# Ring products of channel pairs on two row tiles, the automaton beside its own image's map, and VectorE's gate operations behind a step's taps

## The chip, the cores and the metric

The kernel runs on one core of a Trainium2 chip. A core has TensorE (PE in the profile; PEld are its weight loads), VectorE (DVE), ScalarE (ACT), GpSimd (POOL) and SyncE (SP), and 16 DMA engines. POOL and SP issue the copies here. The metric is the device time of one launch in microseconds (us); lower is better.

## The reference

An input of 32 images, 8 channels, 256 x 256, f32, goes through four layers, each `x = x + layer(norm(x))`. Only layer 0 is touched by the change. With `g` the normalised image it is:

```python
# automaton: a map that is smoothed with a 3x3 kernel per channel, 15 times
grid = drive = g
for _ in range(15):
    mapped = 3.9 * grid * (1.0 - grid)
    local = conv(mapped, K_local, groups=8)
    physics = 0.7 * mapped + 0.3 * local
    grid = 0.85 * physics + 0.15 * drive
cml = clip(grid, 0.0001, 0.9999)
# the map: 3x3 convolution to 128 hidden channels, then 1x1 back to 8
h = relu(conv(g, Wp, bp))
nca = sigmoid(conv(h, Wu, bu))
# the gate: 3x3 convolution of all 24 channels to 8, then 1x1
gin = concatenate([g, cml, nca])
q = sigmoid(conv(relu(conv(gin, Wg1, bg1)), Wg2, bg2))
out = q * cml + (1.0 - q) * nca
```

Layer 1 is a quantized 3x3 convolution (its scale needs the largest value over the whole result of layer 0), layer 2 a plain 3x3 convolution, layer 3 a 5x5 box filter.

## The kernel before, in words

**Layout of the automaton.** Six channels of an image run on TensorE. An image is cut into patches of 16 x 8 pixels, with the 128 pixels of a patch on the partitions and the 512 patches in the free dimension. One step of one channel is two products that add up in one PSUM tile `psc`. `patch_sb` (L391, 128 rows) takes the neighbours inside a patch, and `ring_sb` (L393, 80 rows) those outside it. The 80 ring rows lie in the tile `rings`: the neighbours to the left and right (16 rows each), and for the rows above and below three shifted copies of 8 rows each (24 and 24). They are copied from the tile `state` by four copies on SP (`spread`, L259). VectorE adds the drive (L402, the eviction of a `psc`), and ScalarE squares into `state` (L419). The six channels go in two halves of three, each half with its own `state` and `rings`, and three `psc` buffers in all.

The other two channels run on VectorE in the tile `strip`, with rows of the image on the partitions: nine multiply-adds of 128 x 1024 a step (L338, "taps"; three after the first half's evictions, six after the second's), then L412 and L413. Two copies (`edges`, L263 and L264) exchange the border rows through SP.

**The map and the gate.** `gated()` makes one image's map in 32 batches (`NCH` = 8 blocks n of 4 batches). A batch is four products `ph` from column tiles `im` (L633, evicted to `hh` on ScalarE in L638) and, one batch late, four products of 32 columns into four column strips of `pn` (L610). `im` is loaded from the padded image `xn_d` in DRAM by six copies on POOL a batch (L505), four batches ahead. For each block a gate follows: three groups of products into `pg` (L531, L539 for rows of neighbouring blocks, L543), a ReLU, a product `pq` (L548), a sigmoid into `gt` (L550), and seven VectorE operations (L561 to L568), after which POOL writes the result to `x1_d` (L569). The map's output `nh` stays in SBUF in a ring of eight rows; the gate's halo rows of it are copied from there.

**Order.** The instructions of each engine run in the order in which the program writes them (`manual_schedule`). The automaton of image b (`lattice`) and the map with the gates (`gated`) are generators. Each `yield` of the lattice names a gap in units of about one microsecond of TensorE work, and the loop draws as much work from `gated()`. A step has two halves with 6.3 units each (`BLOCK`). What is drawn beside image b's automaton is the map and the gates of image b - 1. So the first automaton has no map beside it, and the map and gates of the last image run after the last automaton. A third generator, `errands`, writes and loads images and takes the next image's statistics, one piece a half step.

Of the kernel before, what the change touches and what calls it, by code (L numbers as in the profile page):

```python
# [39 lines left out]
    (32, 8, (RB - 1) * PW, 1, -1 - SY, 3, SY),  # L40
    (56, 8, 0, 1, 1 - SY, 3, SY),
)
RING = 80
# [3 lines left out]
HALF = CP // 2  # L47
RQ = 4
BLOCK = 6.3
# [17 lines left out]
def kernel(  # L67
# [100 lines left out]
    with ExitStack() as es:  # L168
# [9 lines left out]
        ring_sb = const(wt, ring, [RING, CP, P], "ring_sb")  # L178
# [41 lines left out]
        nh = wt.tile([P, 8, WP], F32, name="nh")  # L220
        zero = wt.tile([C, WP], F32, name="zero")
        states = [wt.tile([P, HALF, SN], F32, name=f"state{i}") for i in range(2)]
        rings = [wt.tile([RING, HALF, SN], F32, name=f"rings{i}") for i in range(2)]
# [4 lines left out]
        for t in (*xbs, nh, zero, strip):  # L228
            nc.gpsimd.memset(t, 0.0)
        for t in (*states, *rings):  # L230
            nc.gpsimd.memset(t, 0.25)
# [5 lines left out]
        nr_d = [dram.tile([P, HB, WP], F32, name=f"nr_d{i}") for i in range(3)]  # L237

        cr_d = [dram.tile([P, HB, WP], F32, name=f"cr_d{i}") for i in range(3)]
        for t in xn_d:  # L240
            nc.sync.dma_start(
                window(t, 0, [[HP * WP, C], [(HP - 1) * WP, 2], [1, WP]]),
                nh[0:C, 0:2, :],
            )

        def inner(c):

            return states[c // HALF][:, c % HALF, AT : AT + TX * SY].rearrange("p (x y) -> p x y", y=SY)[:, :, 0:TY]

        def spread(half):  # L250

            long = (HALF - 1) * SN + RN
            state = states[half]
            row = state.ap[0][0]
            to = rings[half].rearrange("p c n -> p (c n)")
            for q, n, p, step, far, m, by in RINGS:
                at = p * row + AT + far
                dims = [[step * row, n]] + ([[by, m]] if m > 1 else []) + [[1, long]]
                nc.sync.dma_start(to[q : q + n * m, 0:long], window(state, at, dims))  # L259
# [6 lines left out]
        def errands(b):  # L266
# [3 lines left out]
            if b >= 0:  # L270
                xb = xbs[b % 2]
                for r in four:
                    nc.gpsimd.dma_start(
                        window(
                            xn_d[b % 3], (1 + r.start) * WP,
                            [[HP * WP, C], [RB * WP, HB], [1, 4 * WP]],
                        ),
                        xb[:, r, :].rearrange("p r w -> p (r w)"),
                    )
                    yield  # L280
# [47 lines left out]
        def lattice(b, ahead):  # L328
# [8 lines left out]
            def tap(dy, dx):  # L337
# [8 lines left out]
            nc.vector.tensor_scalar(  # L346
                flat.rearrange("p (x r w) -> p r x w", x=TX, r=RB),
                xi.rearrange("p r (x w) -> p r x w", w=PW),
                st[:, 0:1], st[:, 1:2], ALU.subtract, ALU.mult,
            )  # L350
            yield 5
            for t4 in range(TX // 4):
# [6 lines left out]
                if t4 == 0:  # L359
                    nc.vector.tensor_scalar(  # L360
                        xi, xi, st[:, 0:1], st[:, 1:2], ALU.subtract, ALU.mult
                    )
                if t4 == 4 and b > 0:
                    store(b - 1)
                if t4 == 1:
# [4 lines left out]
                    edges()  # L370
                yield 1
            dr = flat.rearrange("p (x c y) -> p c x y", x=TX, c=C)
            for c in range(CP):
                nc.scalar.activation(inner(c), dr[:, c], AF.Square, bias=minus)
# [3 lines left out]
                if c == 0:  # L378
                    nc.scalar.mul(d2, d2, BETA_)
                if c % HALF == HALF - 1:  # L380
                    spread(c // HALF)
                yield 1.5
            yield 4
            for step in range(STEPS):
                for half in range(2):
                    mine = range(HALF * half, HALF * half + HALF)
# [272 lines left out]
        with tc.manual_schedule():  # L659
# [15 lines left out]
            for _ in rest:  # L675
                pass
# [366 lines left out]
```

## Time and profile before

| what | value |
|---|---|
| median of 3 runs | 16326.91 us (16326.64 to 16338.44) |
| the profiled execution | 16318.33 us, span 16316.6 us |
| mean granted TensorE clock | 0.961 |
| PE, DVE, ACT, POOL busy | 95%, 72%, 35%, 34% of the span |
| DMA | 2276 MB, 1057742 packets |
| start of the first and of the last image's automaton | 33.8 and 12927.2 us |

The busy share of an engine is an average over very different stages. Layer 0 takes the first 13593 us, the other layers the rest, and within layer 0 the first automaton and the last map have stages of their own. A busy PE isn't a PE at its peak, as records overlap: what a product costs is read from the starts of records that follow each other. Idle time of an engine that isn't the bound costs nothing.

### The profile page before, as it was taken

To read this page: it belongs to the slowest core of one execution; us is meant where nothing else is said; L and a number is where in the kernel's file an instruction comes from. 1 tells how busy PE (TensorE), PEld (TensorE's weight loads), DVE (VectorE), ACT (ScalarE), POOL (GpSimd) and SP (SyncE) were. 2 spreads that over 40 slices of the span, in tenths; PEclk is the share of its full clock that TensorE was granted. 3 is DMA by queue.
4 is the path that set the end of the run, shared out by engine and by line. 5 is a ranking of instruction groups with operands and counts; after the bars stand their busy time and mean duration, and the time that the engine had idled before them with its cause. 6 is when DMAs were issued, how large, how long until landed. Compare 5 with 4: busy or idle time off the path is not lost.

```text
span 16316.6 us, 141125 instructions
## 1 busy us (share of the span) xinstructions
PE 15452.2 (95%) x42888; PEld 6215.7 (38%) x42888; DVE 11705.9 (72%) x14652; ACT 5726.7 (35%) x8862; POOL 5598.2 (34%) x9491
## 2 busy tenths in 40 slices
PE   6999999999999999999999999999999997999999
PEld 2333333333333333333333333333333332333333
DVE  7777777777777777777777777777777764555554
ACT  2433444443434434443434444343444442111110
POOL 1333333333333333333333333333333342111111
PEclk7999999999999999999999999999999998999999
DMA  4766666666666666666666666666666664555554
GB/s 104 148 146 144 150 147 144 147 150 146 149 144 148 150 147 147 144 147 145 147 142 149 148 144 147 141 148 146 147 149 147 146 134 98 119 119 119 119 118 105
DMA packets 1057742, 2276.12 MB, mean 139 GB/s; under 512 B 419740, under 2 KB 623508, under 8 KB 1050724
## 3 DMA queue, kind: packets, MB, share of 16 engines
q0 software_dynamic: 704512, 1492.80, 40.6%
q1 hardware_dynamic: 352484, 774.29, 23.4%
q8 instruction: 356, 5.83, 0.2%
q14 instruction: 390, 3.19, 0.1%
HBM read 1078.04 MB, written 471.38 MB: 95 GB/s over the span
## 4 chain that ended last, share of the span: by engine, by line
PE 74%; DVE 13%; DMA 7%; ACT 3%; issue 2%; SPq 1%; POOL 0%; DVEq 0%; ACTq 0%; POOLq 0%
PE ph L633 17%; PE psc L391 14%; PE psc L393 13%; PE pg L531 9%; DVE acc L338 7%; PE psv L725 5%; PE pn L610 5%; PE psv L811 4%; DMA qb<-qh 3%; DMA rings<-state 2%; PE psv L729 2%; PE pq L548 1%; PE pg L543 1%; PE pg L539 1%; DVE psc L402 1%
## 5 line engine op out<-in xcount | busy, mean ns | idle before, releaser
L338 DVE SCALAR_TENSOR_TENSOR acc<-strip,taps_sb,acc 128x1024 f32<-128x1024 f32 x3840 | 4930.4, 1284 | 124.8 <-DMA strip<-strip 4.7
L505 POOL DMA_DIRECT2D im<-xn_d x6144 | 3458.3, 566 | 3250.0 <-PE ph L633 1434.7
L633 PE MATMUL ph<-im,wp_sb 72*128 72x512 f32 x8192 | 4091.7, 615 | 308.8 <-ACT hh L638 251.3
L638 ACT ACTIVATE hh<-ph,bp_sb 128x512 f32<-128x512 f32 x4096 | 2755.8, 690 | 4441.9 <-PE ph L633 4385.7
L402 DVE SCALAR_TENSOR_TENSOR psc<-psc,flat 128x512 f32<-128x512 f32 x2880 | 1921.4, 696 | 2813.0 <-PE psc L393 2797.2
L391 PE MATMUL psc<-state,patch_sb 128*128 128x512 f32 x5760 | 2812.0, 626 | 74.1 <-ACT state L419 63.3
L393 PE MATMUL psc<-rings,ring_sb 80*128 80x512 f32 x5760 | 2713.5, 607 | 129.8 <-DMA rings<-state 129.8
L633 PEld LDWEIGHTS ph<-im,wp_sb 72*128 72x128 f32 x8192 | 1489.5, 193 | 2425.4 <-issue 1587.8
L419 ACT ACTIVATE state<-psc,minus 128x512 f32<-128x512 f32 x2688 | 1690.2, 690 | 1818.8 <-DVE psc L402 1713.1
L391 PEld LDWEIGHTS psc<-state,patch_sb 128*128 128x128 f32 x5760 | 1114.5, 199 | 1696.2 <-issue 1375.7
L393 PEld LDWEIGHTS psc<-rings,ring_sb 80*128 80x128 f32 x5760 | 1114.7, 194 | 1576.8 <-issue 1545.7
L569 POOL DMA_DIRECT2D x_d<-xc x256 | 146.9, 574 | 3493.1 <-DVE xc L564 3416.6
L811 PE MATMUL psv<-xr,w_sb 128*128 128x512 f32 x2560 | 1162.9, 600 | 1.3 <-DVE xr L792 1.3
L610 PE MATMUL pn<-hh,wu_sb 128*32 128x512 f32 x8192 | 1133.9, 609 | 3.3 <-ACT hh L638 3.3
L776 POOL DMA_DIRECT2D x_d<-x x512 | 321.0, 643 | 1941.0 <-DVE x L770 1696.3
L725 PE MATMUL psv<-xh,w_sb 128*128 128x512 f32 x1536 | 753.0, 629 | 9.6 <-issue 9.6
L531 PE MATMUL pg<-xq,wg_sb 128*128 128x512 f32 x1536 | 749.3, 626 | 0.0
L754 ACT ACTIVATE x<-psv,b_sb,sc 128x512 f32<-128x512 f32 x256 | 199.3, 779 | 1466.2 <-PE psv L729 1465.8
L531 PE MATMUL pg<-cq,wg_sb 128*128 128x512 f32 x1536 | 713.7, 601 | 0.0
L811 PEld LDWEIGHTS psv<-xr,w_sb 128*128 128x128 f32 x2560 | 466.1, 189 | 610.8 <-issue 606.0
L338 DVE SCALAR_TENSOR_TENSOR acc<-strip,taps_sb,d 128x1024 f32<-128x1024 f32 x480 | 613.2, 1277 | 0.0
L831 DVE TENSOR_TENSOR y<-psv,y 128x512 f32<-128x512 f32 x256 | 177.1, 692 | 593.7 <-PE psv L811 593.7
(163 smaller groups left out, 12188.9 us busy)
## 6 DMA issues: line engine op xcount, KB each, us to landing
im<-xn_d POOLq DMA_DIRECT2D x6144, 96.6 KB, 6.6
rings<-state SPq DMA_DIRECT2D x1920, 159.5 KB
rings<-state SPq DMA_DIRECT2D x1920, 106.3 KB
strip<-strip SPq DMA_DIRECT2D x960, 126.0 KB
xn_d<-xb POOLq DMA_DIRECT2D x128, 516.0 KB, 7.7
nr_d<-xb POOLq DMA_DIRECT2D x128, 516.0 KB, 7.2
xq<-nr_d POOLq DMA_DIRECT2D x128, 516.0 KB, 5.1
cq<-cr_d POOLq DMA_DIRECT2D x128, 516.0 KB, 7.9
```

Source lines behind the costliest of these rows:

```text
L338: nc.vector.scalar_tensor_tensor(acc, strip[:, dy : dy + RQ, dx : dx + W], taps_sb[:, 3 * dy + dx : 3 * dy + dx + 1], d2 if dy == 1 and dx ...
L391: nc.tensor.matmul(pss[-1], patch_sb[:, c, :], inner(c), start=True, stop=False)
L393: nc.tensor.matmul(pss[c % HALF], ring_sb[:, c, :], rings[half][:, c % HALF, 0 : TX * SY].rearrange("p (x y) -> p x y", y=SY)[:, :, 0:TY], ...
L402: nc.vector.scalar_tensor_tensor(ps, ps, FLOOR, dr[:, c], ALU.max, ALU.add)
L419: nc.scalar.activation(inner(c), pss[c % HALF], AF.Square, bias=minus)
L505: nc.gpsimd.dma_start(im[24 * dy : 24 * dy + 24, k, 0:run], window(xn_d[b % 3], at, [[HP * WP, C], [1, 3], [1, run]]),)
L531: nc.tensor.matmul(o, wg1_sb[:, s, dx, :], src[:, :, dx : dx + W], start=s == dx == 0, stop=False,)
L610: nc.tensor.matmul(pn[32 * q : 32 * q + 32, :], wu_sb[:, i, :], hh, start=i == 0, stop=i == 3,)
L633: nc.tensor.matmul(ph.rearrange("p (k w) -> p k w", w=W), wp_sb, im[:, :, j * WP : j * WP + W], start=True, stop=True,)
L638: nc.scalar.activation(hh, ph, AF.Relu, bias=bp_sb)
L725: nc.tensor.matmul(o, w[:, dx, :], src[:, 2 * i : 2 * i + 2, dx : dx + W], start=dx == 0, stop=False,)
L811: nc.tensor.matmul(pss[k].rearrange("p (c w) -> p c w", w=W), w3_sb[:, dx, :], xr[:, k, mine, dx : dx + W], start=dx == 0, stop=stop,)
```

## The change

**Ring products.** The rings have no shifted copies any more except for the four corners: 16 + 16 rows (left, right), 8 + 8 (above, below), and four rows for the corners above and below: 56 in all. The rings of channel j lie at partitions 0 to 55 and those of channel j + 3 at 64 to 119 of one tile, and the two products of such a pair follow each other, one from each half of the partitions, into two `psc` tiles. A step has three pairs. Pairs 0 and 1 share `state` and `rings` tiles of set 0, pair 2 has set 1. A set is spread by 12 copies, so a step issues 24.

**Step order.** After a pair's products come its two evictions, two, three or four taps, and small gaps of map work: 0.8 before and 0.8 after the two squares of pairs 0 and 1, 0.8 and 8.6 with pair 2. A step's gaps still add up to 12.6.

**VectorE's gate operations.** They are put into a list `spare` and emitted by `work`: four after a step's last tap, some between the transposes of an image. The write to `x1_d` and an image's statistics follow through `follow()`.

**Own image's map.** The image is normalised in place first, written to `xn_d` at once, and copied to `flat` from there. Image b's map now runs beside image b's automaton, and the gates follow about one image (31 batches) later. `place` holds both back: 28 of an image's batches before the next image begins. The map's output goes through DRAM (`nh_d`), and the gate loads it, like its other inputs, in quarters `nq` with halos.

In the diff a line of "..." marks what is left out.

```diff
 RINGS = (
     (0, 16, PW - 1, PW, -SY, 1, 0),
     (16, 16, 0, PW, SY, 1, 0),
-    (32, 8, (RB - 1) * PW, 1, -1 - SY, 3, SY),
-    (56, 8, 0, 1, 1 - SY, 3, SY),
+    (32, 8, (RB - 1) * PW, 1, -1, 1, 0),
+    (40, 8, 0, 1, 1, 1, 0),
+    (48, 2, (RB - 1) * PW, PW - 1, -1 - SY, 2, 2 * SY),
+    (52, 2, 0, PW - 1, 1 - SY, 2, 2 * SY),
 )
-RING = 80
+RING = 56
+LOW, HIGH = 0, 64
 CP = 6
-HALF = CP // 2
+PAIRS = CP // 2
+SETS = ((0, 2), (2, 1))
-BLOCK = 6.3
+BLOCK = 12.6
...
+        def spread(i):
+            long = (SETS[i][1] - 1) * SN + RN
+            to = rings[i].rearrange("p c n -> p (c n)")
+            for state, base in zip(states[i], (LOW, HIGH)):
+                row = state.ap[0][0]
+                for q, n, p, step, far, m, by in RINGS:
+                    at = p * row + AT + far
+                    dims = [[step * row, n]] + ([[by, m]] if m > 1 else []) + [[1, long]]
+                    nc.sync.dma_start(
+                        to[base + q : base + q + n * m, 0:long], window(state, at, dims)
+                    )
...
-            nc.vector.tensor_scalar(
+            nc.vector.tensor_scalar(xi, xi, st[:, 0:1], st[:, 1:2], ALU.subtract, ALU.mult)
+            nc.vector.tensor_copy(
                 flat.rearrange("p (x r w) -> p r x w", x=TX, r=RB),
                 xi.rearrange("p r (x w) -> p r x w", w=PW),
-                st[:, 0:1], st[:, 1:2], ALU.subtract, ALU.mult,
             )
+            for r in range(0, RB, 4):
+                nc.gpsimd.dma_start(
+                    window(
+                        xn_d[b % 3], (1 + r) * WP, [[HP * WP, C], [RB * WP, HB], [1, 4 * WP]]
+                    ),
+                    xb[:, r : r + 4, :].rearrange("p r w -> p (r w)"),
+                )
...
+            taps_of = (((1, 0), (1, 1)), ((1, 2), (0, 0), (0, 1)), ((0, 2), (2, 0), (2, 1), (2, 2)))
             for step in range(STEPS):
-                for half in range(2):
-                    mine = range(HALF * half, HALF * half + HALF)
+                for j in range(PAIRS):
+                    i = j // 2
+                    mine = (j, PAIRS + j)
...
+                    for ps, base in zip(pss, (LOW, HIGH)):
                         nc.tensor.matmul(
-                            pss[c % HALF], ring_sb[:, c, :],
-                            rings[half][:, c % HALF, 0 : TX * SY].rearrange(
+                            ps, ring_sb[base : base + RING, j, :],
+                            rings[i][base : base + RING, j - SETS[i][0], 0 : TX * SY].rearrange(
                                 "p (x y) -> p x y", y=SY
                             )[:, :, 0:TY],
                             start=False, stop=True,
                         )
...
-                    for dy in (1,) if half == 0 else (0, 2):
-                        for dx in range(3):
-                            tap(dy, dx)
+                    for dy, dx in taps_of[j]:
+                        tap(dy, dx)
...
-                    yield 1.7
+                    yield 0.8
                     if step < STEPS - 1:
-                        for c in mine:
-                            nc.scalar.activation(inner(c), pss[c % HALF], AF.Square, bias=minus)
-                        spread(half)
-                        if half == 1:
+                        for c, ps in zip(mine, pss):
+                            nc.scalar.activation(inner(c), ps, AF.Square, bias=minus)
+                        if j == SETS[i][0] + SETS[i][1] - 1:
+                            spread(i)
+                        if end:
                             edges()
-                    next(ahead, None)
-                    yield BLOCK - 1.7
+                    if end:
+                        work(4)
+                    else:
+                        next(ahead, None)
+                    if j == 1:
+                        follow()
+                    yield BLOCK - 4.0 if end else 0.8
...
+        def work(k):
+            for _ in range(min(k, len(spare))):
+                spare.pop(0)[1]()
+
+        def follow():
+            for n, parts in list(after.items()):
+                if next(parts, True):
+                    del after[n]
...
+                while spare and spare[0][0] <= n - 3:
+                    work(1)
...
-                    for name, t in (("xq", nr_d), ("cq", cr_d)):
+                    for name, t in (("xq", nr_d), ("cq", cr_d), ("nq", nh_d)):
...
+                nc.gpsimd.dma_start(nh_d[b % 3][:, 2 * r2 : 2 * r2 + 2, :], nhs[n % 2])
...
-                due.setdefault(batch + 5, []).append(gate(n, quarter))
+                due.setdefault(batch + BATCHES - 1, []).append(gate(n, quarter))
...
             for b in range(B):
                 ahead = errands(b)
-                for gap in lattice(b, ahead):
-                    if b > 0:
-                        left += gap
-                        while left > 0 and place[0] < b * NCH:
-                            left -= next(rest)
-                        left = min(left, 0.0)
+                place[1] = BATCHES * b - 1
+                for k, gap in enumerate(lattice(b, ahead)):
+                    if b == k == 0:
+                        next(rest)
+                    left += gap
+                    while left > 0 and place[0] < place[1]:
+                        left -= next(rest)
+                    left = min(left, 0.0)
```

In the changed kernel the ring products stand in L410, the patch products in L408, the evictions in L418, L412 and L413 in L428 and L429, and the map's products in L684.

## The prediction

> **What bounds the kernel now.** I read the page's busy shares and slices first, then the time by stages, then the instructions of some 8 us in order of time, and last who waited for whom.
>
> ```profile
> PE 15452.2 (95%) x42888; PEld 6215.7 (38%) x42888; DVE 11705.9 (72%) x14652; ACT 5726.7 (35%) x8862; POOL 5598.2 (34%) x9491
> ...
> PE   6999999999999999999999999999999997999999
> ...
> PEclk7999999999999999999999999999999998999999
> ```
>
> TensorE (PE) is the bound in all but the first slice and one near the end. The time by stages (columns: stretch, its length, busy time and instruction count of PE, PEld, DVE, ACT, POOL, then clock, DMA share, GB/s) shows the first automaton alone, the steady state, and the stretch after the last automaton:
>
> ```profile
> 34.00:389.00 355.00, 227.61 (x459) 96.40 (x460) 286.42 (x304) 73.99 (x114) 29.66 (x46) 0.75 0.43 91
> ...
> 4000.00:8000.00 4000.00, 3852.11 (x10844) 1537.69 (x10842) 3010.68 (x3514) 1600.03 (x2503) 1527.31 (x2628) 0.96 0.67 145
> ...
> 13340.00:13600.00 260.00, 249.28 (x781) 91.55 (x779) 60.34 (x111) 113.02 (x163) 147.07 (x251) 0.98 0.50 121
> ```
>
> In the steady state PE is busy 96% and VectorE (DVE) 75%. The starts of L346, one for each image, run from 33.8 to 12927.2 us: 347.9 us from the first to the second, then 402.7, then 416 to 423. Over the 31 images after the first (the last one ends with its transposes at 13343) the mean is 418.1 us. The map of the last image runs alone to 13593, which is 250 us; layers 1 to 3 take the other 2723.
>
> What one product costs is read from the order of time (columns: start, us, engine, line, operation, count):
>
> ```profile
> 4001.14 2.74 PE L393 MATMUL psc<-rings,ring_sb 80*128 80x512 f32 x6
> ...
> 4003.72 1.02 PE L633 MATMUL ph<-im,wp_sb 72*128 72x512 f32 x2
> ...
> 4004.67 1.07 PE L610 MATMUL pn<-hh,wu_sb 128*32 128x512 f32 x8
> ...
> 4005.66 1.98 PE L633 MATMUL ph<-im,wp_sb 72*128 72x512 f32 x4
> ...
> 4007.58 0.62 PE L539 MATMUL pg<-above,wgh_sb 72*32 72x512 f32 x1
> ...
> 4008.56 1.13 PE L543 MATMUL pg<-nh,wg_sb 128*128 128x512 f32 x2
> ```
>
> Each f32 product is two records, 0.43 us apart (six in 2.58 us: 4001.14 to 4003.72), so 0.86 us. The L610 group, four products in four column strips, holds PE for 0.99 us (4004.67 to 4005.66), not 3.44; the two strips of L539 for 0.98. Its neighbours pay too: L633 to L610 is 0.95 where 0.86 was due, and the four L633 records after it take 1.92, not 1.72, which holds 0.11 for a weight load that isn't ahead and 0.09 for the next switch. So a side-by-side group costs 0.86 + 0.31 us.
>
> **The Trainium skill.** "TensorE: Matmul & The Clock Gate", Part 3 (packing small matmuls), says that products in distinct row groups run concurrently, and gives 3.07 times for four row tiles. "TensorEngine Tiling (Array Packing)", Key Properties, says that a change of tiling mode drains TensorE. The trace agrees for column strips (3.44/1.17 = 2.9 times for four, 0.31 us for switching); it holds no row tiles, so for these the pages are all there is. The same page's "PSUM Bottleneck" warns that what evacuates PSUM may be next: the trace has that margin, below.
>
> **The change, part by part.**
>
> *Ring products.* 2880 products of 80 rows (L393) become 1440 pairs of 56 rows at partitions 0 and 64. An image has 45 pairs. A pair costs 1.72 us now. Side by side: 0.86 + 0.31, and 0.08 for two loads of 128 weight columns (0.19 us each in the rows of L393) in place of 32 (0.11): 1.25. Saved 0.47 x 45 = 21.2 us an image. Bounds: 1.07 (only as much as L539) gives 29; 1.45 (both loads exposed) gives 12.
>
> *Step order.* Three pairs instead of two halves. In a step DVE has 9 taps x 1.284, 6 evictions x 0.697, L412 0.697 and L413 1.227: 17.7 us. The gate's seven operations (0.67 to 0.69 each) now follow a step's taps, four at most: 2.8, in all 20.4. Statistics of the next image add 1.7 in four steps: 22.1. Steps now start 24.3 us apart (mean of the L412 intervals); with 3 x 0.47 less, 22.9. DVE fits, and gate operations no longer stand ahead of evictions, which is what lies behind much of this:
>
> ```profile
> PE ph L633 <- ACT hh L638: 157.1, 77, 4.9
> PE psc L393 <- DMA rings<-state: 65.7, 21, 6.1
> ```
>
> (Waits of PE from 4000 to 12000 us: total, times, longest.) That is 8 us an image that could go; but pairs now stand only 1.6 units of map work (some 1.8 us) apart with three psc buffers, so a late eviction reaches PE sooner. I book 0, with 8 us either way.
>
> *Ring copies.* SP issues 24 a step instead of 8, beside 2 strip copies. Now:
>
> ```profile
> 4003.71 0.83 SPq L263 DMA_DIRECT2D strip<-strip  x1
> ...
> 4007.23 14.55 SPq L259 DMA_DIRECT2D rings<-state  x8
> ...
> L259 SPq DMA_DIRECT2D rings<-state x3840: 549/727/3873, 47.5 to 13302.7; - x192
> ```
>
> An issue takes 0.55 to 0.73 us. New: 24 x 0.6 + 1.6 = 16 of 22.9 us; SP has room. Bytes fall from 160 rows of 6.8 KB a step to 112 of 4.5 or 2.2 KB. The tightest loop is set 0: from pair 0's ring product to pair 1's squares 8.3 us (two ring pairs 2.5, the map work between 1.8, pair 1's patch products 1.7, its evictions 1.4, the last square 0.7, hand-overs 0.2), twelve issues 7.2, landing; then the next step's ring product. In the DMA records the last packet of a half's four copies ends 7.0 us after the last issue (median; 5.4 to 9.5 for 5% to 90%), for copies of 24 rows that move in a file; the new ones have at most 16 rows. With 4 to 7 us the loop takes 19.5 to 22.5 of 22.9: hidden, by little. Booked 0. If that cover went, every us would count 15 times an image.
>
> *POOL.* The gate's third input goes through DRAM: 8 writes and 4 loads of 516 KB an image more, and fewer small halo copies. POOL issues 9536 copies in the program instead of 9472, it is busy 38% of the steady state, and the loads are issued four batches (some 40 us) ahead of use, against landings of 5 to 10 us: 0. DMA share falls by the ring bytes and rises by these: about even.
>
> *Own image's map.* L346 and L360 (2.40 + 2.41 us) change places; the xn_d writes follow. Map columns of the new image are asked for in batch 29 and used in batch 32: behind three or four batches and gate pieces, some 30 us, against 2.4 (normalise) + 2.5 (issue) + 7.7 (landing) + 3.4 (issue) + 6.6 (landing) = 23. Hidden: 0. The first automaton now has 28 map batches beside it: 370 us instead of 347.9, from 8 steps of 23 and 7 of 20.3 (the interval of the lone steps) and some 45 ahead. After the last, 8 gates remain: 8 x 9.65 us of PE is 77, plus 18 for what is left over and some 35 for the first loads and the last chain: 130 instead of 250.
>
> *Sum.* 36 (start) + 370 + 31 x (418.1 - 21.2) + 130 + 2723 = 15563 us of span. The profiled execution took 16318.3 for a span of 16316.6, and the median of the runs is 8.6 above it: 15572, say 15570. Pairs of 1.07 to 1.45 us alone give 15320 to 15850, the 8 us either way 250; taken as independent, 15220 to 15950.
>
> **Rivals.**
> *Half overlap.* A product is two passes, and passes start in order: the second tile's first pass could come with the first tile's second. Three passes: 1.29 + 0.31 = 1.60; 5.4 us saved, images of 412.7, total 16060. Against it: the two L539 products, issued one after the other, start 4007.58 and 4007.59.
> *No overlap (ends slower).* Row tiles take turns, and the switch is still paid: 1.72 + 0.31 = 2.03 a pair, 14 us more an image, 432; with 385 first: 16680. It decides from 1.79 us a pair, where images last 421 and the time is that of before. For it: no row tile in the trace. Against it: the skill, and the column strips.
> *The ring loop on SP (also slower).* Twelve issues at 0.78 and a landing of 9.5 us make the loop 27.2 us a step: 15 x 4.3 more an image, 461, total 17570. It decides from issue and landing of 16 us together (steps of 24.5, images of 421). For it: 26 issues in place of 10 in an in-order queue, strips behind rings. Against it: fewer bytes and no copy of 24 rows.
> *The change does little:* all overlap but stalls of 21 us an image eat it, leaving 0.6% from the two ends (16230).
>
> **Chances.** Main case 0.64, half overlap or stalls of like size 0.14, within 0.2% (what a measurement of this kernel can tell from no change) 0.03, the two slower ones 0.19. Faster 0.78, same 0.03, slower 0.19. The range: 15100 (both favourable bounds at once would be 15070) to 16500, which takes in the second case and the nearest of the slower ones. The main case's own range is 15220 to 15950.
>
> **What would show it.** Right: L410 records start in twos, a pair holds PE some 1.1 us, L428 starts lie near 22.9 us apart, images near 397, PE's waits for rings stay below 10 us an image, and layer 1 starts some 120 us sooner after the last automaton. Wrong: L410 passes in single file; a large "PE psc <- DMA rings"; DVE above 90% with PE waiting for squares; PE waiting for im at an image's start.

## Result, and the profile after

The changed kernel takes 16044.5 us (median of 4 runs, 16013.6 to 16076.6). The kernel before, run beside it, takes 16326.8. The ratio is 0.9827, with a 95% interval from 0.9814 to 0.9839. The forecast was 15570 us: the direction is right and the time lies in the range, but of the 757 us forecast only 282 came.

The profiled execution has a span of 16042.5 us. Its page shows the busy shares, the slices of TensorE and the granted clock:

```profile
PE 15001.2 (94%) x42888; PEld 5437.6 (34%) x42888; DVE 11572.5 (72%) x14652; ACT 5754.6 (36%) x8864; POOL 5667.6 (35%) x9558
...
PE   7999999999999999999999999999999997999999
...
PEclk9999999999999999999999999999999998999999
```

The steady state of the kernel after, by stage (stretch, length, busy time and count of PE, PEld, DVE, ACT, POOL, then clock, DMA share, GB/s):

```profile
4000.00:8000.00 4000.00, 3784.99 (x11025) 1329.06 (x11021) 3027.74 (x3563) 1637.58 (x2546) 1587.12 (x2720) 0.96 0.61 147
```

TensorE does less work, and it is also busy less: 95% of this stretch instead of 96%. The stretch now waits. The order of time shows what a pair costs, and what SyncE does meanwhile:

```profile
4009.72 1.02 PE L408 MATMUL psc<-state,patch_sb 128*128 128x512 f32 x2
4010.67 1.13 PE L410 MATMUL psc<-rings,ring_sb 56*128 56x512 f32 x4
4011.73 1.13 PE L588 MATMUL pq<-g,wg_sb 128*128 128x512 f32 x2
...
4020.47 15.79 SPq L272 DMA_DIRECT2D rings<-state  x23
4020.50 1.13 PE L408 MATMUL psc<-state,patch_sb 128*128 128x512 f32 x2 [0.33 <-ACT state L435]
```

The four records of a pair's two ring products hold TensorE for 1.06 us (4010.67 to 4011.73), and the switch before them adds 0.09 (4009.72 to 4010.67 is 0.95, where two records take 0.86). The two tiles run side by side: in the trace their first records start 0.007 us apart. SyncE, though, spends 15.79 us in one stretch on 23 ring copies, 0.69 us each.

Who waits for that? Waits of PE, DVE and ACT over the whole span (total us, times, longest):

```profile
PE psc L410 <- DMA rings<-state: 212.6, 78, 6.3
...
DVE acc L342 <- DMA strip<-strip: 387.4, 140, 7.7
...
ACT state L435 <- DMA rings<-state: 369.0, 143, 8.7
```

In the kernel before, VectorE waited 4.7 us for strips in all, and ScalarE 85.4 us for ring copies to have read `state`. TensorE's own wait for rings was already there:

```profile
PE psc L393 <- DMA rings<-state: 129.8, 37, 18.9
```

From the starts of TensorE's records one can work out, for 29 images of the steady state, how much of an image is the shortest usual distance between two records (the 15th percentile for each pair of lines; records that start within 0.1 us of each other count as one) and how much is waiting beyond it. The waiting can be put down to the automaton's steps:

| kernel | image, us | products | waiting | step 0 | step 1 | step 3 | step 4 | step 12 | step 13 |
|---|---|---|---|---|---|---|---|---|---|
| before | 418.7 | 385.3 | 33.4 | 8.6 | 6.4 | 0.6 | 0.4 | 7.5 | 0.5 |
| after | 414.0 | 365.3 | 48.7 | 10.4 | 5.6 | 3.3 | 6.4 | 0.6 | 5.3 |

So 20.0 us an image were saved, and 15.3 came back as waiting. Other ways of counting records move this split by some 5 us, but not the image, and hardly the steps. Steps 0 and 1 wait in both kernels. The wait of step 12 has gone, and what is new sits in steps 3, 4 and 13, with about 1 us in most of the others. In steps 3, 4 and 13 VectorE waits 8.3 us an image for strips and ScalarE 7.2 us for ring copies; TensorE's own waits there are mostly for relus and sigmoids that come late, and hardly for rings.

A wait costs more than its length. In this stretch of the changed kernel, TensorE waits for a ring of step 0:

```profile
4154.69 2.04 PE L410 MATMUL psc<-rings,ring_sb 56*128 56x512 f32 x2 [6.32 <-DMA rings<-state]
4156.66 3.78 PE L684 MATMUL ph<-im,wp_sb 72*128 72x512 f32 x4
...
4169.48 1.98 PE L684 MATMUL ph<-im,wp_sb 72*128 72x512 f32 x4
```

```profile
4153.10:4163.20 10.10, 8.51 (x15) 2.38 (x16) 3.17 (x3) 3.11 (x5) 6.60 (x12) 0.50 0.91 258
```

After the wait four L684 records take 3.78 us instead of 1.98, and the granted clock is 0.50 for some 10 us. The traces show such stretches at half clock for 27.5 us an image in the kernel before and 32.2 us in the changed one. As products take twice as long in them, they cost up to half of that; the table counts this as waiting.

### The profile page after: what moved, and what is told of

Its sections match the earlier page's. It is cut to its first block, busy times and chain, and to the rows that moved or that the text cites. A ratio compares the mean times of both kernels' runs of the same rounds, so it can differ in the third digit from the quotient of the medians.

```text
span 16042.5 us, 158554 instructions
## 1 busy us (share of the span) xinstructions
PE 15001.2 (94%) x42888; PEld 5437.6 (34%) x42888; DVE 11572.5 (72%) x14652; ACT 5754.6 (36%) x8864; POOL 5667.6 (35%) x9558
## 5 line engine op out<-in xcount | busy, mean ns | idle before, releaser
L342 DVE SCALAR_TENSOR_TENSOR acc<-strip,taps_sb,acc 128x1024 f32<-128x1024 f32 x3840 | 4925.9, 1283 | 485.2 <-DMA strip<-strip 387.4
L684 PE MATMUL ph<-im,wp_sb 72*128 72x512 f32 x8192 | 4269.2, 635 | 269.3 <-ACT hh L689 126.5
L689 ACT ACTIVATE hh<-ph,bp_sb 128x512 f32<-128x512 f32 x4096 | 2758.0, 688 | 3778.2 <-PE ph L684 3726.1
L418 DVE SCALAR_TENSOR_TENSOR psc<-psc,flat 128x512 f32<-128x512 f32 x2880 | 1871.5, 693 | 2524.4 <-PE psc L410 2517.8
L408 PE MATMUL psc<-state,patch_sb 128*128 128x512 f32 x5760 | 2931.1, 623 | 163.0 <-ACT state L435 157.6
L435 ACT ACTIVATE state<-psc,minus 128x512 f32<-128x512 f32 x2688 | 1723.7, 689 | 3137.9 <-DVE psc L418 2756.2
L684 PEld LDWEIGHTS ph<-im,wp_sb 72*128 72x128 f32 x8192 | 1439.8, 195 | 2677.8 <-issue 1971.7
L410 PE MATMUL psc<-rings,ring_sb 56*128 56x512 f32 x5760 | 1805.7, 650 | 230.9 <-DMA rings<-state 212.6
L408 PEld LDWEIGHTS psc<-state,patch_sb 128*128 128x128 f32 x5760 | 1041.7, 194 | 1904.1 <-issue 1249.6
L410 PEld LDWEIGHTS psc<-rings,ring_sb 56*128 56x128 f32 x5760 | 485.4, 187 | 1436.0 <-issue 1037.1
L571 PE MATMUL pg<-cq,wg_sb 128*128 128x512 f32 x1536 | 772.8, 642 | 0.0
L562 POOL DMA_DIRECT2D xc<-xr_d x256 | 145.7, 569 | 1554.5 <-DVE ext L603 673.2
```

What stands on the lines that cost most here:

```text
L342: nc.vector.scalar_tensor_tensor(acc, strip[:, dy : dy + RQ, dx : dx + W], taps_sb[:, 3 * dy + dx : 3 * dy + dx + 1], d2 if dy == 1 and dx ...
L408: nc.tensor.matmul(pss[-1], patch_sb[:, c, :], inner(c), start=True, stop=False)
L410: nc.tensor.matmul(ps, ring_sb[base : base + RING, j, :], rings[i][base : base + RING, j - SETS[i][0], 0 : TX * SY].rearrange("p (x y) -> ...
L418: nc.vector.scalar_tensor_tensor(ps, ps, FLOOR, dr[:, c], ALU.max, ALU.add)
L435: nc.scalar.activation(inner(c), ps, AF.Square, bias=minus)
L571: nc.tensor.matmul(o, wg1_sb[:, s, dx, :], src[:, :, dx : dx + W], start=s == dx == 0, stop=False,)
```

## Experiments

The theories. **Queue:** 24 ring copies and two strip copies stand one behind another on SyncE; late rings hold TensorE, late strips hold VectorE. **Squares:** ScalarE's order puts relus ahead of a pair's squares, so that `psc` buffers come free late. **Backlog:** VectorE's evictions set the pace. Times are medians. Runs made together share their runs of the kernel before, whose medians lie between 16295 and 16318 us; differences of 30 us between groups mean nothing.

**1. Without the corner copies.** In `spread`:

```diff
-                for q, n, p, step, far, m, by in RINGS:
+                for q, n, p, step, far, m, by in RINGS[:4]:
```

> The eight corner copies of a step (two of the six of each side and each set of pairs) are left out, so that the corner neighbours keep their first value: part of the computation is missing, the matmuls keep their shapes. SyncE issues 16 ring copies a step instead of 24, a third less, and the strip copies stand behind fewer. If the rings' and strips' lateness made the gain small (theory queue): ring products wait 4 us an image instead of 12.8, VectorE waits for strips half as long, squares wait less for the copies that read their state; an image goes from 413.7 to about 404, the kernel to 15700 to 15800. If ScalarE's order did it (theory squares): the second patch product still waits 11 us an image, and the time stays within 50 us of 16045. If VectorE's backlog did it: no change either.

Measured: 15127.7 us, ratio to before 0.9277 (0.926 to 0.9294). That is 917 us less than the changed kernel, three times what theory queue expected. A wait of VectorE, the ring products' group (busy and mean, then idle before them and its releaser) and the steady state of this run:

```profile
DVE acc L342 <- DMA strip<-strip: 11.7, 13, 2.5
```

```profile
L410 PE MATMUL psc<-rings,ring_sb 56*128 56x512 f32 x5760 | 1647.8, 644 | 4.3 <-DMA rings<-state 4.2
```

```profile
4000.00:8000.00 4000.00, 3912.27 (x11879) 1385.88 (x11878) 3288.30 (x3904) 1767.65 (x2748) 1690.01 (x2900) 1.00 0.64 153
```

The waits for rings fall from 212.6 to 4.2 us, those for strips from 387.4 to 11.7; PE is busy 98% and the clock is 1.00. An image takes 382.8 us, with 21.0 of waiting; step 0 has 1.6 instead of 10.4 of it, step 4 has 0.7 instead of 6.4. Two things make the gain larger than the waits of TensorE for rings. What stands behind a late copy waits too: ScalarE's wait for ring copies falls from 369.0 to 65.2 us. And the stretches at half clock fall from 32.2 to 3.2 us an image, which is up to 14.5 of the 31.2 us.

Not all of these 31.2 us are a loss by the change. Step 0 gets shorter by 9.7 us (33.4 to 23.7) and step 1 by 6.3 (29.1 to 22.8), and in the kernel before these two steps lasted 31.4 and 29.5 us. So about half of the gain lies in steps that were as slow before the change.

**2. Ring products not neighbours.** The loop over a pair's channels takes patch and ring product of one, then of the other:

```diff
-                    for c in mine:
+                    for c, base in zip(mine, (LOW, HIGH)):
...
-                    for ps, base in zip(pss, (LOW, HIGH)):
```

> The four products of a pair in another order: patch product and ring product of the first channel, then those of the second. The two ring products are no longer neighbours, so the row tiles cannot run beside each other; copies, buffers and all other orders stay. If the row tiles do overlap and TensorE is what an image waits for: a pair's ring products take 1.72 or more instead of 1.17 us, 0.55 to 0.7 us by 45 pairs = 25 to 31 us an image, time 16800 to 17050. If the image is set by queues and VectorE and TensorE's saving has gone into its own waits (theory queue): less than half comes back, 16200 to 16500. If the tiles had not overlapped: no change.

Measured: 16884.1 us, ratio 1.0354 (1.0328 to 1.0379), 840 us more than the changed kernel and slower than before. In the order of time of this run each product now starts 1.05 us after the one before it:

```profile
4019.64 1.12 PE L410 MATMUL psc<-rings,ring_sb 56*128 56x512 f32 x2
4020.69 1.13 PE L409 MATMUL psc<-state,patch_sb 128*128 128x512 f32 x2
4021.75 1.12 PE L410 MATMUL psc<-rings,ring_sb 56*128 56x512 f32 x2
```

The run takes away more than the overlap: every product pays a change of row tiles, 0.19 us above 0.86. Four products take 4.2 us instead of 2.9, which by 45 pairs would be some 60 us an image; 24 were felt (438.3 against 414.0), as the slower steps gave the copies time: waits for strips fell from 387.4 to 44.6 us. The overlap is real. A run without it whose products do not pay that change each time was not made.

**3. Squares first.** The gap goes behind the squares:

```diff
-                    yield 0.8
                     if step < STEPS - 1:
...
-                    yield BLOCK - 4.0 if end else 0.8
+                    yield BLOCK - 3.2 if end else 1.6
```

> The gap of 0.8 of gated work between a pair's VectorE operations and its squares is moved behind the squares, so that no relu or sigmoid of the gated batches is put ahead of them on ScalarE. Theory squares: the second patch product of the next pair no longer waits for a buffer (11.4 to about 4 us an image), the image goes from 413.7 to 405 to 408, the kernel to 15780 to 15880. Theory queue: the patch products' wait is the same or moves to the ring products, within 60 us of 16045. It could also be slower: the gap was what gave the gated batches work while VectorE was still at the pair; without it the squares stand at the head of ScalarE's queue and hold back the relu (up to 16200).

Measured: 16176.6 us, ratio 0.9918 (0.9897 to 0.9939), 132 us slower than the changed kernel. ScalarE's waits in this run:

```profile
ACT state L434 <- DVE psc L418: 4713.4, 1233, 12.2
ACT hh L688 <- PE ph L683: 1778.7, 1646, 31.5
```

In the changed kernel these two are 2756.2 and 3726.1: ScalarE now stands at squares whose evictions aren't done, with relus behind them. The gain that theory squares expected did not come; the gap was in the better place.

**4. Strips issued by GpSimd.** In `edges`, for both copies:

```diff
-            nc.sync.dma_start(strip[...
+            nc.gpsimd.dma_start(strip[...
```

> The two strip copies of a step are issued by GpSimd instead of SyncE; ring copies stay. Theory queue in the form that the strips behind 24 ring copies delay VectorE, and by it the adds, squares and patch products: VectorE's wait for strips falls from 12 to 2 us an image, an image is 4 to 6 us shorter, the kernel 15850 to 15930. If only the ring copies count: the copies of set 0 come two issues earlier at most, 16000 to 16045. If GpSimd's own order holds the strips back (the loads of the gated batches stand in the same queue): slower, up to 16300.

Measured: 15967.0 us, ratio 0.979 (0.9766 to 0.9814), 78 us faster. That lies between the two theories. VectorE's wait for strips falls to 1.7 us, and the waits of steps 3, 4 and 13 go with it (3.3, 6.4 and 5.3 us become 0.6, 0.7 and 1.3). So the strips behind 24 ring copies were what these steps waited for. But 8.3 us more come up in step 5 and 3.9 in step 10, where rings are late: TensorE waits 261.5 us for them instead of 212.6. What GpSimd's queue has to do with that stays open.

**5 to 7. Who issues.** Three runs move copies off SyncE. All data are still moved.

```diff
-                    nc.sync.dma_start(
+                    (nc.sync if q < 48 else nc.scalar).dma_start(
```

is the first; in the second the corners go to `nc.gpsimd`, and in the third all copies of the HIGH side go to `nc.scalar`.

> All 24 ring copies of a step are made, so the data moved are those of the changed kernel; the eight corner copies are issued by ScalarE, behind the squares they read, and SyncE issues the other 16. Theory queue (what counts is the number of issues that stand one behind another on SyncE, each with its lane to wait for): most of the 917 us that leaving the corners out brought comes here too, less what ScalarE pays for eight issues of 0.6 us a step (4.9 us a step; ScalarE is busy 36%): 15200 to 15500. Theory traffic (the corner copies' data or their packets slow the other transfers): no gain, 16000 to 16100. Theory ScalarE: issues ahead of relus and sigmoids hold TensorE back as much as the rings did: 15900 to 16300.

> As the one with the corners on ScalarE, but GpSimd issues the eight corner copies. Theory queue: GpSimd (busy 35%) can take them, 15300 to 15700; but they stand in order with the loads of the gated batches, whose bursts come in four steps of an image, so that in those steps the corner rows come late: up to 16100. Theory traffic: no gain, 16000 to 16100.

> The twelve copies of a step for the HIGH side are issued by ScalarE, the twelve of LOW by SyncE. Theory queue: SyncE's chain is halved (8.4 to 4.2 us for a set of pairs) and ring products do not wait; ScalarE pays 12 issues of 0.6 us a step, 7.4 us, and is then busy 36 + 32%: 15200 to 15600. Theory ScalarE: squares and relus late behind issues: 15900 to 16300.

Measured: corners on ScalarE 16925.7 us, ratio 1.0376 (1.0355 to 1.0396); on GpSimd 15621.7, ratio 0.9583 (0.9562 to 0.9603); the HIGH side on ScalarE 20031.7, ratio 1.2286 (1.2263 to 1.2309). Theory queue missed the first by over 1400 us, and even theory ScalarE by over 600; both missed the third by over 3700. ScalarE's own order of time in the run with the corners shows why:

```profile
4038.69 4.32 ACTq L272 DMA_DIRECT2D rings<-state  x4
4043.05 1.84 ACT L689 ACTIVATE hh<-ph,bp_sb 128x512 f32<-128x512 f32 x3 [5.44 <-DMA rings<-state]
```

Four issues hold it for 4.32 us, and three relus stand behind them. (Four issues elsewhere in this trace take 2.72 us; that the rest is a wait for earlier copies to land is likely, not shown.) TensorE no longer waits for rings in this run (2.1 us) but 504.2 us for relus. GpSimd, which evicts nothing for TensorE, carries the same copies and brings 423 us. VectorE's wait for strips in that run:

```profile
DVE acc L342 <- DMA strip<-strip: 26.5, 26, 2.9
```

An image takes 398.3 us, close to the forecast of 396.9. Steps 3, 4 and 13 no longer wait (0.6, 0.7 and 1.3 us), while steps 0 and 1 still do (10.1 and 4.5), as in the kernel before. All data still move, so these 423 us come from where the eight copies are issued; whether they also land sooner from GpSimd was not separated.

**8. The gate's operations at once.** One part of the change undone: behind `spare.extend(...)` of a gate follows

```diff
+                work(7)
```

> One part of the change undone: VectorE's seven operations of a gated batch are emitted as soon as the batch's sigmoid is, as before the change, not behind a step's taps; ring products, queues and buffers as changed. Theory queue: these operations are not what the image waits for; within 80 us of 16045. Theory backlog (VectorE's evictions set the pace and the gate operations ahead of them cost as in the kernel before): +5 to +10 us an image, 16200 to 16400.

Measured: 16301.0 us, ratio 1.0 (0.9989 to 1.001), 256 us slower than the changed kernel; an image takes 421.0 us instead of 414.0. TensorE's largest wait in this run, and one of its instances:

```profile
PE ps L109 <- DVE mv L106: 364.6, 35, 27.5
...
3938.81 0.56 PE L109 MATMUL ps<-mv,gavr_sb 128*128 128x1 f32 x2 [9.71 <-DVE mv L106]
```

The time is what theory backlog expected, but the cause is another. This is the small product that averages the statistics of a finished image of layer 0 (its weights are `gavr_sb`). In this run it stands right behind the VectorE operation that it needs, 0.5 us after that one's start, and TensorE waits about 10 us at it in every image. In the changed kernel that operation is done 17 us ahead, and in the kernel before, too, L104, the same product, hardly waited (47.9 us in 5 waits, 29.7 of them in one). Against the changed kernel TensorE waits 324 us more here and 136 more at patch products, and 191 less for relus and sigmoids. So the run does not price the place of the gate's operations as the kernel before had it.

**9. Small corner copies.** 24 issues as in the changed kernel, with 8 elements a row in the corners:

```diff
+                    short = long if q < 48 else 8
+                    dims[-1][1] = short
...
-                        to[base + q : base + q + n * m, 0:long], window(state, at, dims)
+                        to[base + q : base + q + n * m, 0:short], window(state, at, dims)
```

> SyncE issues all 24 ring copies, but the eight corner copies move 8 elements a row instead of 1122 or 543: the corner neighbours keep their first value for the rest, so part of the computation is left out. The number of issues is that of the changed kernel, the corner copies' data are gone. Leaving the corners out brought 917 us, handing them to GpSimd 423. Theory issue (SyncE's time per issue and the order on its queue are what count): within 150 us of 16045. Theory landing (a corner copy's four rows of 4.5 KB, each a single packet on one DMA engine, land late and hold the lanes that later issues wait for): 15130 to 15400. In between if both count.

Measured: 15900.9 us, ratio 0.9755 (0.9741 to 0.977), 144 us faster than the changed kernel. So without the corners' data 144 of the 917 us come, and the other 773 only when their issues go too. SyncE's issues in the changed kernel and in this run (minimum, median, maximum in ns):

```profile
L272 SPq DMA_DIRECT2D rings<-state x11520: 542/654/3492, 68.9 to 13173.3; - x199
```

```profile
L274 SPq DMA_DIRECT2D rings<-state x11520: 545/654/3004, 72.0 to 13011.5; - x199
```

For the corner copies alone the median is 0.654 us in both runs, whether a row has 32 bytes, 2172 or 4488.

**10 to 12. The image's start.** `errands` starts with four empty turns, so that the next image's loads come two steps later: first alone, then with the corners on GpSimd. The third run has the corners on GpSimd and 9.0 units instead of 5.5 ahead of step 0.

```diff
+                for _ in range(4 if b >= 0 else 0):
+                    yield
                 xb, d2 = xbs[(b + 1) % 2], d2s[(b + 1) % 2]
```

> The changed kernel, but the four loads of the next image and its two channels of d2 start two steps later (four empty turns ahead of them, where the kernel before had four stores); everything after them in that chain moves two steps too. Theory burst (steps 0 and 1 hold 17 us of TensorE's 54 us of waiting an image because these loads, the stores of the normalized image and the loads of a quarter fall together with the first two spreads): 4 to 10 us an image, 15720 to 15920. Theory count (SyncE's issues alone set it): within 60 us of 16045. Loss possible: the wait moves into steps 2 and 3 and the next image's statistics come later: 16100.

> Corner copies issued by GpSimd (15622 us alone) and the loads of the next image two steps later. What is left in steps 0 and 1 of the run with corners on GpSimd is 15 us an image, of which 2 to 3 are left anyway. Theory burst: GpSimd's queue is free of the four loads then, 8 to 12 us an image, 15230 to 15370. Theory count: no change, 15560 to 15680.

> Corner copies issued by GpSimd, and 9 units of gated work instead of 5.5 between the last scaling and step 0, so that the first spread has some 3.5 us more cover. If the wait of the pair-0 ring products in step 0 (4.2 us an image) only lacks cover: minus 3 us an image, 15500 to 15570, unless it comes back because the gated batches run out earlier at the image's end. If GpSimd stands in a queue of loads: the corners are later than that and nothing changes, 15580 to 15680.

Measured: 15958.5 us, ratio 0.9791 (0.9776 to 0.9806); **15494.2 us, ratio 0.9506 (0.9491 to 0.952)**; and 15778.2, ratio 0.9684 (0.967 to 0.97). Late loads bring 86 us alone and 127 with the corners on GpSimd, less than theory burst expected both times. Alone, the wait left step 1 (5.6 to 0.7 us) and over half of it came back in step 3 (3.3 to 6.4). More cover, that is more other work between a copy's issue and its use, made it 157 us slower than corners on GpSimd, which neither theory expected: step 0's wait went from 10.1 to 1.6 us, step 1's from 4.5 to 12.8. Each time most of the wait moved instead of going away.

**13 and 14. Which set counts.** Corners left out for one set only, `RINGS[: 6 if i == 0 else 4]` and the reverse.

> The four corner copies of set 1 (pair 2) are left out, those of set 0 stay: part of the computation is missing. SyncE issues 20 ring copies a step. Theory first set (only the twelve issues of set 0, which stand before the next step's first ring product, count): strips come 2.8 us earlier and little else, 15850 to 16000. Theory loop (24 issues and two strip copies are a chain near the step's 24 us, so that a burst on the DMA engines makes it overrun): a third to a half of the 917 us, 15550 to 15750.

> The four corner copies of set 0 (pairs 0 and 1) are left out, those of set 1 stay: part of the computation is missing. SyncE issues 20 ring copies a step. Theory first set: set 0 is issued in 5.6 instead of 8.4 us, the waits of pair 0's ring products go and with them most of the 917 us, 15200 to 15450. Theory loop: the same as without set 1's corners within 100 us, 15550 to 15750.

Measured: without set 1's corners 15736.4 us, ratio 0.9658 (0.9644 to 0.9673); without set 0's 15316.7, ratio 0.9398 (0.9384 to 0.9412). TensorE's wait for rings, first without set 1's corners, then without set 0's:

```profile
PE psc L410 <- DMA rings<-state: 237.3, 95, 5.3
```

```profile
PE psc L410 <- DMA rings<-state: 14.8, 12, 2.1
```

Four issues less in set 1 take 308 us away (VectorE's wait for strips falls to 21.4), four less in set 0 take 728. Each of the two theories fits one of the runs. Steps 3, 4 and 13 get shorter in both (25.3, 27.2 and 27.2 us become 22.0, 21.6 and 23.2, and 23.5, 21.8 and 23.2). Steps 0 and 1 get much shorter only without set 0's corners (33.4 and 29.1 become 25.0 and 25.4), whose issues stand between a step's second pair and the next step's first ring products. The two add up to more than 917, so each relieves part of what the other does.

**15 to 18. Sharing the corners.** All with late loads. The corners of an image's first spread issued by ScalarE, the others by GpSimd; only the HIGH side's corners on GpSimd; and of the first spread only set 0's four on ScalarE, or two of these on SyncE and two on ScalarE.

> Corners on GpSimd and the next image's loads two steps later (15494 us), but the corners of an image's first spread are issued by ScalarE: eight issues an image there. If step 0's 9 us are corners that stand behind the loads of a quarter on GpSimd's queue: minus 4 to 8 us an image less 5 us of ScalarE's time that is only partly felt, 15300 to 15450. If step 0 waits for landings in a burst of traffic on the DMA engines, whoever issues: 15470 to 15560.

> Loads two steps later, the corners of the LOW side on SyncE, those of the HIGH side on GpSimd: 20 and 4 issues a step. Theory loop with slack: SyncE has enough with four issues less and GpSimd's bursts hold back only half as many, 15350 to 15480. Theory that each issue on SyncE costs about the same: half way between the two, 15650 to 15800.

> As the run with the first spread's corners on ScalarE (15491 us), but only set 0's four are issued there; set 1's four, which are wanted three products later, go to GpSimd. In the profile ScalarE stood 5 us behind set 1's four issues with a relu next in line, and TensorE waited for it. If that is the 10 us an image ahead of step 0: minus 4 to 8 us an image, 15250 to 15370. If the wait comes back in step 0 at pair 2 or in step 1: 15450 to 15520.

> As the one before, but of set 0's four corner copies at an image's start two are issued by SyncE and two by ScalarE. If ScalarE's issue time is the rest of what is lost there: 0 to 40 us faster than the one before. If SyncE's ten issues in a row bring the ring wait in step 0 back: 50 to 150 us slower than the one before.

Measured: 15490.7 us, ratio 0.9504 (0.949 to 0.9518); 15568.3, ratio 0.9553 (0.9537 to 0.9569); 15554.0, ratio 0.9549 (0.9528 to 0.9569); 15515.2, ratio 0.9522 (0.9503 to 0.9541). None clearly beats corners on GpSimd with late loads, and the second and third lie outside what was expected of them. The order of time of the first of them, at an image's start:

```profile
4002.03 4.30 ACTq L272 DMA_DIRECT2D rings<-state  x4
4006.38 0.69 ACT L691 ACTIVATE hh<-ph,bp_sb 128x512 f32<-128x512 f32 x1 [4.97 <-issue]
```

The 9 us that left step 0 (10.5 to 1.4) came back as 10 ahead of it (1.6 to 11.5), behind such issues. With only four copies on ScalarE it was 5.3 ahead of step 0, 1.4 in it and 9.1 in step 1. What is left at an image's start, some 10 us, was only moved about; the kernel before had it too. Which of the transfers there is the one to move stays open.

## Why the prediction was right or wrong

**Ring products: right, a little small.** Booked 1.25 us a pair and 21.2 us an image; measured 1.06 and 0.09 for the switch, which by 45 pairs is 25.7 us. The count of all products shows 20.0 saved; where the rest went it does not say. "Half overlap" and "no overlap" are out. The Trainium skill's "TensorE: Matmul & The Clock Gate", Part 3, says that distinct row groups run concurrently; two tiles of 56 rows here agree.

**Ends: right.** The first automaton took 371.6 us (370 booked), from the last transposes to the gate's last operation it was 121 us (130), layers 1 to 3 took 2718 (2723).

**Step order: open on one side, a loss on the other.** "I book 0, with 8 us either way." The two lines shown there come to 11.6 us an image, not 8. What the gate's new place brings was not measured: experiment 8 makes a wait that the kernel before did not have. The fear beside it, that closer pairs meet late evictions, is seen: patch products wait 12.3 us an image instead of 5.5, 7.0 of it ahead of a pair's second one. Most of this stays with the corners on GpSimd (11.8), so it is not the ring copies, and moving the squares ahead does not help it.

**Ring copies: this is the step that failed.** "With 4 to 7 us the loop takes 19.5 to 22.5 of 22.9: hidden, by little. Booked 0." For the loop itself that was nearly so. Twelve issues of set 0 take 8.4 us in the median, not 7.2, and the landing after them 2.5. From the first issue to the last packet that is 11.1 us, below what I had allowed: in most steps the copies are in time. But a quarter of the spreads take over 14.0 us and a tenth over 17.1, and the cover is 14.6 (22.9 less the 8.3 worked out). The long ones come where GpSimd's copies keep the DMA engines busy: 69 and 77% of the time in the first two spreads of an image (19.0 and 16.4 us in the median), 66 to 67% in those ahead of steps 3, 9 and 14 (13.0, 13.7 and 16.7 us), 0 to 46% in the others. That the one comes of the other was not tried by itself. I had measured the cover against the middle of the spread times and booked nothing for the tail. Yet TensorE's wait for rings grew only from 129.8 to 212.6 us, and stayed below the 10 us an image that I had named as a sign of being right.

What cost the time is the other half of the step. "SP has room" counted SyncE's time, 16 of 22.9 us. What matters is what stands behind what in its queue: VectorE waited 387.4 us for strips behind both sets instead of 4.7, and ScalarE 369.0 us for ring copies that still read `state`, ahead of its squares, instead of 85.4. TensorE then waits for relus and sigmoids, above all in steps 3, 4 and 13; by experiment 4 it is the strips that count there. With the eight corner copies of a step issued by GpSimd these waits go, and 423 of the missing 474 us come (15622 against 15570 forecast). The waits of steps 0 and 1, by contrast, were already in the 418.1 us from which I started (15.0 us an image before, 16.0 after).

**The rival on SyncE** named the right queue, with the wrong form. It made every step 4.3 us too long and gave 17570 us; in fact some steps are late by much and most by little. It deserved to be spread out over the main case, as a loss of some 16 us an image, not set beside it with a small chance.

**The balance.** An image was to take 396.9 us and takes 412.9 (31 images, from the second one's start to the last transposes). Better than booked: 4.5 us (pairs). Worse: the 15.7 us that handing the corners to GpSimd takes away (414.0 to 398.3), and some 6 us of patch products. That is 17 the wrong way against 16 observed; the terms come from separate runs and counts and need not add so well.

## What to carry to other kernels

Count what one queue issues between the last producer and the first consumer, multiply by the measured time of an issue, add the landing, and compare the slow tenth of that, not its middle, with the cover. Then list everything else that stands behind these copies in the same queue, or waits for them to have read their source. Before a wait is put down to a change, look whether the kernel before had it at the same place. A packing that makes matmuls cheaper by splitting their operands into more copies is paid for on the issuing queue: here 550 of the 917 us came when GpSimd issued the corner copies and some loads moved two steps. Here such copies did well on an engine that evicts nothing, and badly on the one that frees PSUM buffers for TensorE.

## What the hardware showed that I had not expected

- A change of row tiles around every product costs 0.19 us of TensorE each time (1.05 instead of 0.86 us, experiment 2), the same order as the whole gain of packing if the order of products is badly chosen. In that run's trace a product's weights are loaded only when it starts (4019.64 us for both); among the 80-row products of the kernel before, they were loaded 0.43 us ahead.
- The issue of a copy costs 0.56 to 0.69 us on SyncE (medians of its forms), and for the corner copies the bytes made no difference. The Trainium skill's "DMA: Bandwidth & Descriptors", section "Issuing engines are not separate DMA queues", says that issuing from several engines saves only sequencer time, usually small beside the transfer; here 24 issues at 0.65 us fill 15.7 of 24 us, and moving eight of them is worth 423 us of 16044.
- In these traces ScalarE did nothing else while it issued or waited to issue: twelve copies a step made the kernel 25% slower than the changed one, with a mean granted clock of 0.855 instead of 0.960.
- A wait of a few us can be paid twice. Behind the 6.32 us wait shown above, products took twice as long for some 10 us. At half clock stood 32.2 us of an image in the changed kernel, 18.0 with the corners on GpSimd, 3.2 without the corners, and 170.2 in the run with twelve copies on ScalarE.
